# Layer norm gate moved between a selective scan and its product on VectorE

## Chip, cores and metric

The kernel runs on one core of a Trainium2 chip. The metric is the device time of one execution in microseconds. Times of the kernel before are given as the median of three runs; one more execution was profiled.

## Reference

The input is x of shape (2, 256, 256, 128) in float32. Two layers follow, each on the group-normalised x and each added to it. The first is a row attention; the change does not touch it. The second is a selective scan model with 256 inner channels, 16 states and 65,536 tokens per image:

```python
xz = x @ in_proj_w.T
xi, z = jnp.split(xz, 2, axis=-1)
xi = jax.nn.silu(conv3x3_depthwise(xi) + conv_b)
...
# selective_scan, for each channel d and state n along the tokens:
h = dA_t * h + dBx_t
y_t = sum over n of h * c_t
...
y = (y - mu) * jax.lax.rsqrt(var + 1e-05) * ln_g + ln_b     # over the 256 channels
y = y * jax.nn.silu(z)
return y @ out_proj_w.T
```

## The kernel before

The attention comes first (lines 269 to 575) and leaves its sum in DRAM. The second layer is the scan stage. It goes through 128 **steps** (64 per image); a step covers R = 4 rows of 256 tokens, that is T = 1024 tokens.

A step has NU = 32 **units**. The 128 partitions of a unit hold 32 channels times 4 states. The 32 units are 8 groups of channels times 4 groups of states. For unit t the engines do this, each with one instruction:

- `decay(t)` (line 958, ScalarE): da = exp(delta * a), into PSUM. There are two buffers, da0 and da1.
- `drive(t)` (line 968, GpSimd): hb = du * bb, for two units at once.
- `scan(t)` (line 980, VectorE): h = da * h + hb along the tokens. For most units it writes h over da in PSUM; for pooled units it writes h over hb in SBUF.
- `product(t)` (line 995, VectorE): yc = h * cc. In the five pooled pairs, which start at units 6, 14, 22, 26 and 30, the product is done on GpSimd for the pair (line 1004); unit 11 has its product on GpSimd alone.
- `add_up(t)` (line 1027, TensorE): for every four units, 32-column matmuls that add the states of yc into y in PSUM. It frees the yc buffers; the pool has four pairs.
- `remember(t)` (line 985, ScalarE): copies the last column of h to the state kept for the next step.

So VectorE runs scan, product, scan, product, with two scans and no product at a pooled pair.

Between the units run pieces of two other jobs. `project(k)` prepares a later step: transposes, the convolution as nine matmuls (line 678), the gate z (line 704), silu of both, and softplus. ScalarE does each silu or softplus as one pass of 2048 elements with a table load on both sides; they stand at units 12 (softplus, line 765), 20 (silu of z, line 720) and 28 (silu of xs, line 697). `finish_row` finishes one row of the step before, four rows per step, eight units apart. Its pieces, counted from the row's first unit a, a multiple of 8, are:

- a: `fetch` loads xres and szr (the silu of z) from DRAM, issued by SP.
- a: `turn` (line 830, TensorE) transposes and centres y into yt.
- a + 1 to a + 3: `stats`, `scales` and `norm` on ScalarE (lines 842 to 854) make the normalised row yn.
- a + 4: `back` (line 865, TensorE) transposes yn into yd in PSUM.
- a + 5: `gated` (line 873, VectorE): yg = yd * szr, 128 x 512.
- a + 7: `mix` (lines 877 and 881, TensorE) multiplies with the output projection and adds the residual.
- a + 8: `leave` (line 891, ScalarE) copies the row out, and SP stores it.

The gates of the four rows thus fall at units 5, 13, 21 and 29 of a step, none of them pooled, and each followed by a pooled pair at units 6, 14, 22 and 30. There are 512 gates.

The order on each engine is the order in which the loop at the end issues the pieces; no scheduler changes it within an engine. In a turn of that loop the scan and the product of unit t come first, then the pieces put at t with `at`, those for TensorE last. So the gate stood behind the product of its unit.

## Time and profile before

| what | value |
|---|---|
| median of three runs | 15883.89 us |
| lowest and highest run | 15882.23 and 15885.26 us |
| profiled execution, its own time | 15886.66 us |
| profiled execution, its span | 15884.8 us |
| scan stage in the profiled execution | from about 2680 us to the end |

The profile gives for each engine the time in which it was busy and, for each instruction, its start, its duration and what ended the idle time before it. In a timeline row the first number is the start in microseconds from the start of the span and the second the duration; brackets hold idle time ahead of the instruction and its releaser. In a row of stretches the busy times of the five engines (PE, PEld, DVE, ACT, POOL) are followed by the granted TensorE clock as a share of full speed, the DMA share and GB/s. DVE is VectorE, ACT ScalarE, POOL GpSimd, PE TensorE and PEld its weight load. A row of waits names who waited for whom, the microseconds in total, the number of times and the longest.

### The profile page before, as it was taken

What the parts mean: (1) busy time and instruction counts of PE and PEld (TensorE: products, weight loads), DVE (VectorE), ACT (ScalarE), POOL (GpSimd) and SP (SyncE); (2) the same over time, 40 slices, a digit from 0 to 9 for tenths busy, and PEclk for the clock granted to TensorE, in tenths of its full rate; (3) what the DMA queues carried; (4) which work ended last, traced back from release to release, by engine and by line L of the source; (5) the groups of instructions that cost most, each with busy time, mean ns of one, the idle gap of its engine ahead of it and who ended that gap; (6) DMA issues with size and microseconds to landing.
All of it is one profiled execution on the core that took longest, in us unless ns stands there. A gap on an engine that the chain in (4) does not pass through costs nothing. (4 is left out here: it accounts for less than half of the span.)

```text
span 15884.8 us, 178043 instructions
## 1 busy us (share of the span) xinstructions
PE 13780.9 (87%) x59451; PEld 7002.8 (44%) x59451; DVE 14454.8 (91%) x12356; ACT 10796.7 (68%) x20003; POOL 13328.8 (84%) x3344
## 2 busy tenths in 40 slices
PE   6999998888888888888888888888888888888886
PEld 4877884333333333333333333333333333333333
DVE  7665555999999999999999999999999999999998
ACT  3555554777777777777777677777777777777775
POOL 1111113999999999999999999999999999999998
PEclk8999998999999999999999999999999999999998
DMA  4322222767677767677777667777677767776675
GB/s 188 123 101 86 80 96 105 239 238 245 240 241 242 246 240 240 240 245 241 243 242 244 230 241 242 242 244 244 240 241 241 245 241 243 242 244 240 240 243 185
DMA packets 1428908, 3452.13 MB, mean 217 GB/s; under 512 B 119785, under 2 KB 711185, under 8 KB 1407505
## 3 DMA queue, kind: packets, MB, share of 16 engines
q1 hardware_dynamic: 1427984, 3440.73, 62.6%
q8 instruction: 468, 7.67, 0.2%
q14 instruction: 456, 3.73, 0.1%
HBM read 2752.41 MB, written 687.88 MB: 217 GB/s over the span
## 5 line engine op out<-in xcount | busy, mean ns | idle before, releaser
L968 POOL TENSOR_TENSOR hb<-du_r,bb 128x2048 f32<-128x2048 f32 x2048 | 9243.5, 4545 | 82.3 <-DMA du_r<-du_d 15.7
L980 DVE TENSOR_TENSOR_SCAN da<-da,state,hb 128x1024 f32<-128x1024 f32 x2688 | 6300.4, 2344 | 137.9 <-ACT da L958 134.3
L958 ACT ACTIVATE da<-delta_r,a_neg 128x1024 f32<-128x1024 f32 x4096 | 4580.7, 1118 | 88.9 <-DMA delta_r<-delta_d 10.1
L678 PE MATMUL u_ps<-xn,w_tap 128*128 128x512 f32 x9216 | 4335.3, 612 | 91.3 <-ACT sz L715 73.2
L995 DVE TENSOR_TENSOR yc<-da,cc 128x1024 f32<-128x1024 f32 x2688 | 3291.8, 1225 | 235.9 <-PE y L1027 69.1
L980 DVE TENSOR_TENSOR_SCAN hb<-da,state,hb 128x1024 f32<-128x1024 f32 x1408 | 3233.4, 2334 | 61.5 <-ACT state L985 47.7
L1004 POOL TENSOR_TENSOR yc<-hb,cc 128x2048 f32<-128x2048 f32 x640 | 2909.0, 4545 | 101.0 <-ACT state L985 81.1
L678 PEld LDWEIGHTS u_ps<-xn,w_tap 128*128 128x128 f32 x9216 | 1713.7, 195 | 2453.6 <-issue 1837.9
L1027 PE MATMUL y<-yc,sel 128*32 128x512 f32 x16384 | 2323.6, 689 | 18.5 <-POOL yc L1004 18.1
L435 POOL TENSOR_TENSOR x1g<-xc,bo_all 128x512 f32<-128x512 f32 x256 | 316.0, 1276 | 1840.5 <-DVE stats L484 1839.6
L985 ACT COPY state<-da 128x1 f32<-128x1 f32 x2688 | 425.9, 158 | 1637.5 <-DVE yc L995 1630.1
L830 PE MATMUL yt<-centre,ys 128*128 128x256 f32 x4096 | 1030.9, 395 | 284.7 <-ACT ob L891 284.7
L1027 PEld LDWEIGHTS y<-yc,sel 128*32 128x32 f32 x16384 | 470.2, 121 | 1790.0 <-issue 1646.5
L704 PE MATMUL z_ps<-xn,w_z 128*128 128x512 f32 x1024 | 696.3, 768 | 547.0 <-ACT xn L665 307.3
L746 PE MATMUL dt_ps<-xd,w_dt 8*128 8x512 f32 x1024 | 740.6, 811 | 482.0 <-ACT delta L757 385.6
L385 ACT ACTIVATE e<-s_ps,nmx 128x256 f32<-128x256 f32 x1024 | 477.6, 476 | 967.7 <-DVE nmx L376 960.0
L985 ACT COPY state<-hb 128x1 f32<-128x1 f32 x1408 | 268.5, 191 | 1242.7 <-DVE hb L980 1242.6
L830 PEld LDWEIGHTS yt<-centre,ys 128*128 128x128 f32 x4096 | 742.0, 191 | 464.4 <-ACT ob L891 381.9
L881 PE MATMUL o_ps<-w_out,szr 128*128 128x128 f32 x4096 | 793.9, 276 | 0.0
L881 PE MATMUL o_ps<-w_out,yg 128*128 128x128 f32 x4096 | 792.8, 275 | 0.0
L352 DVE TENSOR_TENSOR v<-v_ps,bv_all 128x512 f32<-128x512 f32 x256 | 177.1, 692 | 592.1 <-PE v_ps L345 592.1
L775 POOL TENSOR_TENSOR xs<-delta,xs 128x1024 f32<-128x1024 f32 x256 | 606.7, 2370 | 99.1 <-ACT delta L765 99.1
(134 smaller groups left out, 17280.7 us busy)
## 6 DMA issues: line engine op xcount, KB each, us to landing
bb<-bc_d SPq DMA_DIRECT2D x1024, 512.0 KB, 4.0
cc<-bc_d SPq DMA_DIRECT2D x1024, 512.0 KB, 5.3
delta_r<-delta_d SPq DMA_DIRECT2D x1024, 512.0 KB, 6.3
du_r<-du_d SPq DMA_DIRECT2D x1024, 512.0 KB, 5.2
sz_d<-sz SPq DMA_DIRECT2D x128, 1024.0 KB, 6.5
szr<-sz_d SPq DMA_DIRECT2D x512, 256.0 KB, 4.1
xs_d<-xs SPq DMA_DIRECT2D x128, 1024.0 KB, 9.5
xr<-xs_d SPq DMA_DIRECT2D x256, 512.0 KB, 5.9
```

The costliest lines, as they stand in the source:

```text
L678: nc.tensor.matmul(o["u"], w_tap[:, h, tap, :], xn[:, i * RB + dy : i * RB + dy + RB, dx : dx + W], start=(tap == 0), stop=(tap == 8),)
L704: nc.tensor.matmul(o["z"], w_z[:, h, :], xn[:, 1 + i * RB : 1 + (i + 1) * RB, 1 : W + 1], start=True, stop=True,)
L746: nc.tensor.matmul(o["dt"], w_dt[:, h, :], o["xd"][0:DR, i * TB : (i + 1) * TB], start=True, stop=True,)
L830: nc.tensor.matmul(o["yt"][:, j, :], ys[k, h][:, t0 + j * P : t0 + (j + 1) * P], centre[:, (1 - h) * P : (1 - h) * P + DI], start=(h == 0) ...
L881: nc.tensor.matmul(o["o"][:, j, :], o[by][:, h, j * P : (j + 1) * P], w_out[:, i, h, :], start=False, stop=(j == WT - 1 and h == NH - 1 an ...
L958: nc.scalar.activation(da, spreads["delta", k, h, q], AF.Exp, scale=a_neg[:, g, m : m + 1])
L968: nc.gpsimd.tensor_tensor(hb, spreads["pair", k, h, q], repeats["bb", k, h, m].unsqueeze(1).to_broadcast([P, 2, T]), ALU.mult,)
L980: nc.vector.tensor_tensor_scan(u["h"], u["da"], u["hb"], st, ALU.mult, ALU.add)
L985: nc.scalar.copy(st, units[t]["h"][:, T - 1 : T])
L995: eng.tensor_tensor(u["yc"], u["h"], repeats["cc", k, h, m], ALU.mult)
L1004: nc.gpsimd.tensor_tensor(yc, hb, repeats["cc", k, h, m].unsqueeze(1).to_broadcast([P, 2, T]), ALU.mult)
L1027: nc.tensor.matmul(y[q * CQ : (q + 1) * CQ, cols], sel, units[t + q]["yc"][:, cols], start=False, stop=(m == NSG - 1),)
```

## The change

The gate is no longer put into the list of pieces at its unit. It is kept in a dictionary `between`, and the loop calls it after the scan of that unit and ahead of its product. On VectorE the order scan, product, gate becomes scan, gate, product at the 507 gates that have a scan in their unit. For the last five rows there are no more scans, and their gates run alone, as before.

```diff
@@ -605,6 +605,7 @@
     slots = {}
+    between = {}
 
     def at(t, piece, *args, pe=False):
...
@@ -901,11 +902,11 @@
             (2, scales),
             (3, norm),
             (4, back),
-            (5, gated),
             (7, mix),
             (8, leave),
         ):
             at(a + i, piece, pe=piece in (turn, back, mix))
+        between[a + 5] = gated
 
@@ -1068,6 +1069,9 @@
                 decay(t + 1)
             if 0 <= t < end:
                 scan(t)
+            if t in between:
+                between[t]()
+            if 0 <= t < end:
                 if not pooled(t):
                     product(t)
             others, on_pe = slots.pop(t, ((), ()))
```

## Prediction

> **What bounds the kernel now.** I read the page's busy table first, then the waits of VectorE, then its timeline through one step of 32 units, and last the granted TensorE clock in short stretches. Below, "unit n" is the unit with t % 32 = n. A step has four gate products, at units 5, 13, 21 and 29, and there are 128 steps (127 of them with gates among scans).

> ```profile
> PE 13780.9 (87%) x59451; PEld 7002.8 (44%) x59451; DVE 14454.8 (91%) x12356; ACT 10796.7 (68%) x20003; POOL 13328.8 (84%) x3344
> ...
> DVE   7665555999999999999999999999999999999998
> ```

> VectorE is the fullest engine and is full from slice 8 on: that is the scan stage, where the change lies. GpSimd is nearly as full there, but VectorE waits for it hardly at all. The waits of VectorE, of which the scan stage shows these:

> ```profile
> DVE yc L995 <- PE y L1027: 69.1, 129, 2.2
> DVE hb L980 <- ACT state L985: 47.7, 126, 1.0
> DVE yg L873 <- PE yd L865: 43.8, 5, 10.7
> ```

> Two waits come once in every step (129 and 126 times). The gate's own wait for TensorE comes 5 times, all but nothing of it among the scans. The timeline of VectorE and TensorE around a gate at unit 13:

> ```profile
> 8055.84 2.35 DVE L980 TENSOR_TENSOR_SCAN da<-da,state,hb 128x1024 f32<-128x1024 f32 x1
> ...
> 8058.13 0.60 PE L865 MATMUL yd<-ident,yn 128*128 128x128 f32 x4
> 8058.22 1.23 DVE L995 TENSOR_TENSOR yc<-da,cc 128x1024 f32<-128x1024 f32 x1
> ...
> 8059.36 0.68 DVE L873 TENSOR_TENSOR yg<-yd,szr 128x512 f32<-128x512 f32 x1
> ...
> 8059.96 2.34 DVE L980 TENSOR_TENSOR_SCAN hb<-da,state,hb 128x1024 f32<-128x1024 f32 x1
> ```

> Scan to product is 2.38 us, product to gate 1.14, gate to the next scan 0.60: 4.12 in all. The product needs the scan's output and starts after its end. Where the next instruction is independent it starts ahead of the end: the scans of a pooled pair follow each other after 2.26 us (8059.96 to 8062.22). So the dependence costs 2.38 - 2.26 = 0.12 us. TensorE ends yd at 8058.73, 2.89 us after the scan's start and 0.63 us ahead of the gate.

> The wait for y, at unit 28, in three steps (VectorE's timeline):

> ```profile
> 8003.16 1.23 DVE L995 TENSOR_TENSOR yc<-da,cc 128x1024 f32<-128x1024 f32 x1 [0.31 <-PE y L1027]
> ...
> 8105.56 1.22 DVE L995 TENSOR_TENSOR yc<-da,cc 128x1024 f32<-128x1024 f32 x1 [0.31 <-PE y L1027]
> ...
> 8209.45 1.23 DVE L995 TENSOR_TENSOR yc<-da,cc 128x1024 f32<-128x1024 f32 x1 [1.45 <-PE y L1027]
> ```

> The first two are 102.40 us apart. So are most steps to within 0.01 us, which no sum of engine times would give. TensorE's clock says why; the stretches before, in and after its two slow patches of a step:

> ```profile
> 7998.41:8001.83 3.42, 3.21 (x10) 0.90 (x14) 3.42 (x2) 3.11 (x8) 3.42 (x2) 0.50 1.00 338
> 8001.83:8005.24 3.41, 3.41 (x17) 1.17 (x10) 3.10 (x3) 3.38 (x3) 3.41 (x2) 1.00 0.58 180
> 8042.79:8046.20 3.41, 2.04 (x6) 0.69 (x5) 3.38 (x3) 2.61 (x7) 3.33 (x2) 1.00 0.41 121
> 8046.21:8056.44 10.23, 8.64 (x23) 2.00 (x22) 10.04 (x7) 8.52 (x14) 10.15 (x4) 0.50 0.73 249
> 8056.45:8059.86 3.41, 3.41 (x13) 1.68 (x12) 3.38 (x3) 3.32 (x6) 3.41 (x1) 1.00 0.95 303
> ```

> The third column from the right is the granted clock: half speed for 3.4 us ahead of unit 28's y and for 10.2 us ahead of unit 13's yd, full speed around them.

> [...] half-clock stretches of 3.42 and 10.23 us are one and three windows, and 102.40 us is exactly 30 windows. So the step is locked to the clock's windows. [...]

> How the lock works, from the scan starts of all steps. If a step begins later against the windows, TensorE does more of unit 28's y at full clock, and VectorE's wait for it shrinks by half of the shift; if earlier, it grows by half. After a disturbance of 0.35 us (about every 16 steps) the wait jumps to 1.45 us, and the steps take 103.89, 103.35, 102.88, 102.64, 102.52, 102.46, 102.43, 102.41 us: the excess over 102.40 halves each time and sums to 3.4 us, one window. There are 7 or 8 such slips. The wait adds to VectorE's work whatever is missing from 30 windows. yd of unit 13 moves likewise: in those steps it ended 1.48 to 3.13 us after the scan's start.

> **The change, part by part.** Nothing is added or removed: on VectorE 507 of the 512 gates swap places with the product before them; the orders of TensorE, ScalarE, GpSimd and SP stay. SP's szr load loses a wait for VectorE that had long been met: nothing. TensorE's y takes an extra wait for that product, which ended several units earlier: nothing, since that work covers it. SP's szr load (4.1 us to land, issued five units or some 17 us ahead) is there before an earlier gate; if it were not, the gate would hold VectorE for the rest. The product ends 0.60 - 0.12 = 0.48 us later after its scan; behind it wait ScalarE's state copy and decay t+2 (1.12 us), due 2.26 us after the next scan starts: covered, with some 0.9 us left.

> A scan into PSUM followed by an independent instruction does not occur in this trace. Bounds for its pitch: 2.26 us (pooled pair, gain 0.12) and 2.38 (gain 0). No reason excludes a small loss, but the gate has no tie to the scan; I take 2.26.

> - Unit 5: yd is over 3 us early. 2.26 + 0.60 + 1.14 = 4.00 for 4.12: -0.12 us a step.
> - Unit 21: the next scan is held by ScalarE (the 47.7 us): the decay of unit 22 runs from 8085.61 to 8086.73 at the end of a ScalarE chain that began at product 19 (silu and two table loads lie in it), and the scan starts at 8086.83. Saved time becomes wait: 0.
> - Unit 29: yd ends at 8006.32, 0.2 us ahead of 8004.30 + 2.26, where the gate would start: no wait. The next scan's decay ends at 8008.27, and scans start 0.10 us after at the earliest, against 8008.42 now: -0.05; -0.12 once unit 28's wait is longer.
> - Unit 13: yd comes at 2.89, the gate at 2.93 (0.05 from TensorE's end to VectorE's start at unit 28), the product at 3.53, the next scan at 4.67: +0.55 us if the windows stay where they are.

> Sum at today's phase: 0.55 - 0.12 - 0.05 = +0.38 us a step. But then a step is longer than 30 windows and drifts against them. Carrying the halving rules for yd and y from step to step, the drift ends where unit 13's yd is early enough (its scan start plus 1.5 us; the gate is free from 2.2 on) and unit 28's wait has grown. There units 5, 13 and 29 each save 0.12, and the wait at unit 28 grows from 0.24 above its shortest form to 0.24 + 0.36 = 0.60, which lies within the 0.1 to 1.35 seen. The step is again **102.40 us**. The rules give 8 full slips: about +3 us in all.

> Sum against the profiled execution's 15886.66 us (span 15884.8 and 1.9 around it): 15889.6. It lies 2.8 above the median of 15883.89, so I give **15886** for the runs.

> **Rivals.**
> - The late yd stays (slower). Place: gate at unit 13; price +0.38 us x 127 = +48: 15932. It decides if yd ends later than 2.22 us after its scan's start in most steps, or if steps slip a window every 8 instead of 16 (8 more slips x 3.4 = +27: 15911). For it: at today's phase yd is 0.64 late. Against: yd moves with the windows. 13%.
> - The lock breaks (faster): 0.36 x 127 = -46, 15838. It needs y to come earlier with the gates. Against: y hangs on the clock, and the wait took every value from 0.1 to 1.35 while the rest of the step stayed the same. 7%.
> - The swap saves nothing, since the gate too starts 2.38 after the scan: then unit 28's wait stays near 0.24 and the step is again 102.40: 15886. Same number, another mechanism; 15% within the 80%.

> **Numbers.** A measurement tells 0.2%, 32 us, from no change. Within: 80%, slower 13%, faster 7%. The range takes slips lost (7 x 3.4 = 24 below) and ten added (34 above): 15856 to 15920; it leaves out most of the two outer rivals.

> **What would show it.** Right: steps of 102.40 us; a scan at units 5 and 13 followed by the gate after 2.26 us; VectorE's wait for y near 0.7 us at unit 28, some 110 us in total; no regular wait of yg for yd; the wait for ScalarE at unit 22 up by 0.12 a step. The slow patch ahead of unit 13 begins some 0.6 us later after unit 8's scan. Wrong: yg waiting for yd in most steps, steps off 102.40, or slips much more or less often than every 16 steps.

## Result, and the profile after

The changed kernel takes **15856.1 us** (median of 20 runs, 15852.0 to 15861.7) against 15883.7 for the kernel before (20 runs, 15878.4 to 15890.0): a ratio of **0.9982, 95% interval 0.9977 to 0.9988**, 27.6 us or 0.17% faster. The profiled execution took 15853.44 us, its span is 15851.4 against 15884.8.

The busy line of the page and the waits of VectorE that answer to those shown of before:

```profile
PE 13783.1 (87%) x59451; PEld 6983.3 (44%) x59451; DVE 14400.7 (91%) x12356; ACT 10834.7 (68%) x20003; POOL 13333.6 (84%) x3344
```

```profile
DVE yc L996 <- PE y L1028: 90.0, 125, 1.4
DVE hb L981 <- ACT state L986: 65.2, 126, 1.0
DVE yg L874 <- PE yd L866: 45.4, 6, 10.7
```

VectorE is busy 54 us less and waits 38 us more: 21 us more for TensorE's y (69.1 before) and 17 more for ScalarE (47.7 before). The pauses too short to be listed as waits take 17 us less, which with the two others makes the 33 us of span. Among the scans the gate waits for yd once, 0.47 us in step 87 (the first step is step 0). The timeline of VectorE and TensorE around unit 13:

```profile
8039.68 2.35 DVE L981 TENSOR_TENSOR_SCAN da<-da,state,hb 128x1024 f32<-128x1024 f32 x1
8040.66 0.60 PE L866 MATMUL yd<-ident,yn 128*128 128x128 f32 x4
...
8041.93 0.67 DVE L874 TENSOR_TENSOR yg<-yd,szr 128x512 f32<-128x512 f32 x1
...
8042.52 1.21 DVE L996 TENSOR_TENSOR yc<-da,cc 128x1024 f32<-128x1024 f32 x1
8043.66 2.35 DVE L981 TENSOR_TENSOR_SCAN hb<-da,state,hb 128x1024 f32<-128x1024 f32 x1
```

The gate starts 2.25 us after the scan, the product 0.59 later, the next scan 1.14 later: 3.98 us where it was 4.12. And yd now ends 1.58 us after the scan's start (8041.26), where it ended 2.89 after. The product of unit 28 in three steps:

```profile
7987.29 1.23 DVE L996 TENSOR_TENSOR yc<-da,cc 128x1024 f32<-128x1024 f32 x1 [0.72 <-PE y L1028]
...
8089.69 1.23 DVE L996 TENSOR_TENSOR yc<-da,cc 128x1024 f32<-128x1024 f32 x1 [0.72 <-PE y L1028]
...
8192.26 1.23 DVE L996 TENSOR_TENSOR yc<-da,cc 128x1024 f32<-128x1024 f32 x1 [0.56 <-PE y L1028]
```

The first two are again 102.40 us apart, and the wait is 0.72 where it was 0.31: every step takes back what its gates saved. The third is a step with the disturbance of 0.35 us. Before, its wait jumped from 0.31 to 1.45 and a **slip** followed, a step and its successors that together take one clock window more. (A **window** is a measured pitch: in the profile of before the granted clock is 1.00 or 0.50, and all 300 whole stretches at 0.50 begin on one grid of 3.4133 us, to within 1 ns, and last one or several such pitches; 30 of them are 102.40 us.) Now the wait takes up half of the disturbance (0.72 to 0.56), the step is 102.57 us, and the next steps of 102.33, 102.35 and 102.38 us give the rest back.

So where did the 33.4 us of span go? I summed, from the starts of the unit 0 scans, what each step is above 102.40 us:

| steps | before | after |
|---|---|---|
| 1 to 60 | +17.5 us | -0.4 us |
| 61 to 63 (change of image) | +20.1 us | +17.3 us |
| 64 to 126 | +11.1 us | +1.6 us |
| steps over 102.95 us | 20 | 3 |

The first and the third row lose 27.4 us, and most of that are **slips that no longer happen**: eight before (steps 5, 14, 21, 37, 53, 79, 95 and 111), one after (step 87), so seven windows or 23.9 us. The last three steps give 2.0 of the 27.4. A further 2.8 lie at the change of image, the rest of the 33.4 at the two ends. The quiet steps did not become shorter by anything. The granted clock even fell, from a mean of 0.929 to 0.925 over the span.

The regular disturbance is the same in both kernels: VectorE pauses for 0.44 to 0.47 us between a scan and its product, at unit 12 in steps 5, 21, 37 and 53, at unit 18 in steps 79, 95 and 111. All seven brought a slip before, none does after. In step 53 of the changed kernel it reads:

```profile
8141.29 1.23 DVE L996 TENSOR_TENSOR yc<-da,cc 128x1024 f32<-128x1024 f32 x1 [0.44 <-issue]
```

The slip at step 87 began otherwise: the product of unit 12 waited 1.08 us for y, and the gate of unit 13 then waited for yd.

The stretches at half clock (granted clock 0.50) in one step of the changed kernel:

```profile
8030.75:8037.57 6.82, 4.80 (x18) 1.09 (x18) 6.72 (x4) 5.50 (x11) 6.82 (x3) 0.50 0.67 219
8058.06:8061.47 3.41, 3.41 (x14) 0.60 (x16) 3.38 (x3) 2.46 (x5) 3.41 (x1) 0.50 1.00 357
8081.95:8088.77 6.82, 4.35 (x17) 1.10 (x18) 6.82 (x4) 6.12 (x13) 6.82 (x2) 0.50 1.02 360
```

Two, one and two windows, where this step had three and one before: a new one at unit 18, and two windows for one ahead of unit 28. The stretch ahead of unit 13 now ends at 8037.57, 2.11 us ahead of the scan's start, where it ended 0.60 us behind it (8056.44 and 8055.84), and yd is early.

### The profile page after: what moved, and what is told of

Read it like the earlier page. It is cut to its first block, busy times and chain, and to the rows that moved or that the text cites. A ratio compares the mean times of both kernels' runs of the same rounds, so it can differ in the third digit from the quotient of the medians.

```text
span 15851.4 us, 178043 instructions
## 1 busy us (share of the span) xinstructions
PE 13783.1 (87%) x59451; PEld 6983.3 (44%) x59451; DVE 14400.7 (91%) x12356; ACT 10834.7 (68%) x20003; POOL 13333.6 (84%) x3344
## 5 line engine op out<-in xcount | busy, mean ns | idle before, releaser
L679 PE MATMUL u_ps<-xn,w_tap 128*128 128x512 f32 x9216 | 4233.1, 600 | 13.6 <-ACT sz L716 8.9
L679 PEld LDWEIGHTS u_ps<-xn,w_tap 128*128 128x128 f32 x9216 | 1670.3, 190 | 2277.4 <-issue 1852.5
L1028 PE MATMUL y<-yc,sel 128*32 128x512 f32 x16384 | 2414.0, 714 | 17.8 <-POOL yc L1005 17.0
L705 PE MATMUL z_ps<-xn,w_z 128*128 128x512 f32 x1024 | 761.3, 835 | 633.9 <-ACT sz L716 324.8
L747 PE MATMUL dt_ps<-xd,w_dt 8*128 8x512 f32 x1024 | 695.1, 764 | 511.2 <-ACT delta L758 419.4
```

The lines of the kernel that those rows point to most:

```text
L679: nc.tensor.matmul(o["u"], w_tap[:, h, tap, :], xn[:, i * RB + dy : i * RB + dy + RB, dx : dx + W], start=(tap == 0), stop=(tap == 8),)
L705: nc.tensor.matmul(o["z"], w_z[:, h, :], xn[:, 1 + i * RB : 1 + (i + 1) * RB, 1 : W + 1], start=True, stop=True,)
L747: nc.tensor.matmul(o["dt"], w_dt[:, h, :], o["xd"][0:DR, i * TB : (i + 1) * TB], start=True, stop=True,)
L1028: nc.tensor.matmul(y[q * CQ : (q + 1) * CQ, cols], sel, units[t + q]["yc"][:, cols], start=False, stop=(m == NSG - 1),)
```

## Experiments

**Theory 1**: the step is held at 30 windows of TensorE's clock, and the gain is the slips avoided, because the step rests at another point against the windows. **Theory 2**: VectorE's work sets the time, and each of the 507 swaps gives its own share, 27.6 / 507 = 0.054 us. They part as soon as the gates are swapped at one unit only, since theory 2 then gives a quarter each time.

The kernel before was run again beside each group of experiments and took 15883.7 to 15887.9 us there. The ratios are to those runs; between kernels of different groups, a few microseconds say nothing.

### Gates swapped at one unit only

For U = 5, 13, 21 and 29:

```diff
-        between[a + 5] = gated
+        if (a + 5) % NU == U:
+            between[a + 5] = gated
+        else:
+            at(a + 5, gated)
```

> Only the gates of unit 5 stand between scan and product; those of units 13, 21 and 29 stay behind the product. Theory 1 (the step is held at 30 windows of TensorE's clock, 102.40 us, and the whole gain of the change is the window slips that no longer happen): 0.15 us saved a step moves the step 0.3 us away from the point where a disturbance of 0.35 us makes it slip, so almost no slips are left and the whole gain is there: 22 to 28 us below the kernel before, steps still 102.40. Theory 2 (each swap saves its own share, 27.6 us / 507 gates = 0.054 us): 127 x 0.054 = 7 us below.

> Only the gates of unit 13 stand between scan and product. Theory 1: the step has no resting point, because where VectorE's work and the wait at unit 28 would make 102.40 us, yd comes 0.6 us too late for the gate; steps slip a window every two to four steps and the time is 50 to 90 us above the kernel before (slower by 0.3 to 0.6%), with yg waiting for yd in most steps. Theory 2: 7 us below the kernel before.

> Only the gates of unit 21 stand between scan and product. Theory 1: the next scan is held by ScalarE, so the step, its phase and its slips stay as they were: within 3 us of the kernel before. Theory 2: 7 us below.

> Only the gates of unit 29 stand between scan and product. Theory 1: as for unit 5, 20 to 28 us below the kernel before with almost no slips, steps 102.40. Theory 2: 7 us below.

| swapped at | time us | ratio to before (95%) | steps over 102.95 us |
|---|---|---|---|
| unit 5 | 15858.4 | 0.9983 (0.9976 to 0.9989) | 5 |
| unit 13 | 15957.9 | 1.0046 (1.0033 to 1.0058) | 61 |
| unit 21 | 15884.3 | 0.9999 (0.9991 to 1.0007) | 20 |
| unit 29 | 15861.9 | 0.9986 (0.9979 to 0.9992) | 8 |
| all | 15856.1 | 0.9982 (0.9977 to 0.9988) | 3 |

Theory 2 falls. Unit 5 alone gives 26.9 us, the whole gain; unit 29 alone 23.3; unit 21 nothing, and VectorE's wait for ScalarE is 65.7 us there for 47.7; and the same saving at unit 13 costs 72.7 us. The sign depends on the place. With unit 5 alone the wait of unit 28 rests at 0.45 us, and the disturbance takes it to 0.27 without a slip; from 0.31, in the kernel before, the same disturbance brings the slip. With unit 13 alone, the gate waits for yd 38 times in all, 33 of them among the scans, where the kernel before has none and the changed one a single one. The waits of VectorE and the timeline of one such step:

```profile
DVE yc L999 <- PE y L1031: 133.0, 128, 2.2
...
DVE yg L874 <- PE yd L866: 68.6, 38, 9.8
```

```profile
6843.22 2.35 DVE L984 TENSOR_TENSOR_SCAN da<-da,state,hb 128x1024 f32<-128x1024 f32 x1
...
6845.67 0.60 PE L866 MATMUL yd<-ident,yn 128*128 128x128 f32 x4
...
6846.31 0.69 DVE L874 TENSOR_TENSOR yg<-yd,szr 128x512 f32<-128x512 f32 x1 [0.74 <-PE yd L866]
...
6848.04 2.34 DVE L984 TENSOR_TENSOR_SCAN hb<-da,state,hb 128x1024 f32<-128x1024 f32 x1
```

yd ends 3.05 us after the scan's start, so the gate starts 3.09 us after its scan instead of 2.25 (0.74 us of it idle), and the next scan 4.82 us after it instead of 4.12. The steps run 104.25, 103.29, 102.85, 102.63 us and again from the start. The four sum to 413.02 us, which is 121 windows where 120 would be four quiet steps: one slip every four steps. In three of the four the gate does not wait at all; a step of 102.40 us has no place to rest, because where the wait at unit 28 would make it (some 0.45 us), yd ends 3.0 us after the scan, in the kernel before and with unit 5 alone as well. That explains why 33 waits of 0.7 us, 24 us in all, can cost 73: most of it comes as the wait for y, 133.0 us for 69.1, in the same step (1.45 us) and in the next three.

### All but unit 13

```diff
-        between[a + 5] = gated
+        if (a + 5) % NU == 13:
+            at(a + 5, gated)
+        else:
+            between[a + 5] = gated
```

> The gates of units 5, 21 and 29 stand between scan and product, those of unit 13 behind the product. Theory 1: VectorE's work is 0.14 us a step longer than in the changed kernel, and the wait at unit 28 is that much shorter; steps 102.40 us, few slips, 15856 within 6 us. Theory 2: three quarters of the gain, 15863.

Measured: 15854.1 us, ratio 0.9979 (0.9971 to 0.9987), quiet steps of 102.40. The swap at unit 13, harmful alone, gives and takes nothing beside the others that these runs can tell: without it the wait at unit 28 rests at 0.59 us, with it at 0.72.

### Less VectorE work: half a gate

The gate of unit 5 leaves out half of its columns; for these the output projection takes szr in place of yg, so that the other engines keep their work. Once in the changed kernel, once in the kernel before with all gates behind their products:

```diff
-            nc.vector.tensor_tensor(o["yg"], o["yd"], o["szr"], ALU.mult)
+            if (a + 5) % NU == 5:
+                nc.vector.tensor_tensor(
+                    o["yg"][:, 0, :], o["yd"][:, 0, :], o["szr"][:, 0, :], ALU.mult
+                )
+            else:
+                nc.vector.tensor_tensor(o["yg"], o["yd"], o["szr"], ALU.mult)
...
-                    for i, by in enumerate(("yg", "szr")):
+                    first = "szr" if h and (a + 5) % NU == 5 else "yg"
+                    for i, by in enumerate((first, "szr")):
```

> The changed kernel, whose gate at unit 5 computes only its first 256 of 512 columns (in those rows the output projection takes szr in place of yg for the other half): some 0.3 us less work on VectorE in every step. Theory 1 (step held at 30 windows): the wait for y at unit 28 grows by those 0.3 us, steps stay 102.40 us, and the time is that of the changed kernel, 15856 within 5 us. Theory 2 (VectorE's work sets the time): 127 x 0.3 = 38 us less than the changed kernel, 15818.

> The kernel before, all gates behind their products, whose gate at unit 5 computes only its first 256 of 512 columns (the output projection takes szr for the other half in those rows): some 0.27 us less VectorE work a step. Theory 1: the order of gate and product is not what counts; any tenth of a microsecond saved moves the step away from its slip point: 15850 to 15860, 24 to 34 us below the kernel before, steps 102.40. Theory 2: 127 x 0.27 = 34 us below, 15850, with steps of 102.13.

The changed kernel with half a gate: 15849.9 us (ratio 0.9978, 0.9970 to 0.9987), 6 us below the changed kernel where the work saved is 127 x 0.27 = 34 us; it is also 1 us below the range that theory 1 gave. Two successive quiet steps of it on VectorE's timeline:

```profile
6963.18 1.23 DVE L1002 TENSOR_TENSOR yc<-da,cc 128x1024 f32<-128x1024 f32 x1 [0.98 <-PE y L1034]
...
7065.57 1.23 DVE L1002 TENSOR_TENSOR yc<-da,cc 128x1024 f32<-128x1024 f32 x1 [0.98 <-PE y L1034]
```

Again 102.39 apart, and the wait is up from 0.72 to 0.98: the 0.26 us saved lie in it. Summed as above, its steps are 3.9 us shorter in all, in and after the disturbed ones.

The kernel before with half a gate: 15855.1 us (0.9980, 0.9972 to 0.9988), median step 102.398, four steps over 102.95 instead of 20. The time alone fits both theories; the steps decide, since theory 2 wants 102.13. So the order of gate and product is not what counts. Savings of 0.15 to 0.7 us a step that reach the product of unit 28 and meet no late yd brought 23 to 34 us, with little regard to their size.

### More VectorE work: one reduction

```diff
                     product(t)
+                if t % NU == 2:
+                    nc.vector.tensor_reduce(spin, centre[:, 0:P], AX.X, ALU.add)
```

> The changed kernel with one more VectorE instruction a step: a reduction of 128 constant columns behind the product of unit 2, some 0.15 to 0.2 us. Theory 1: the step's resting point moves 0.3 to 0.4 us, past the point where yd of unit 13 comes a window's share later; the gate then waits, and the step slips every four or five steps: 40 to 70 us above the kernel before, that is 70 to 95 us above the changed kernel for 20 to 25 us of work. Theory 2: 20 to 25 us above the changed kernel, about 15879.

Measured: 15945.4 us, ratio to before 1.0038 (1.0026 to 1.0051): 89 us above the changed kernel. The reduction makes unit 2 longer by 0.19 us (3.79 for 3.60), 24 us in all. Where no disturbance comes between, its steps run 104.36, 103.17, 102.79, 102.59, 102.50 and again; the five sum to 515.41 us, 151 windows for 150: a slip every five steps. The gate waits for yd 29 times at unit 13. The waits of VectorE:

```profile
DVE yc L997 <- PE y L1029: 130.0, 127, 1.5
...
DVE yg L875 <- PE yd L867: 65.5, 33, 9.8
```

### TensorE's idle gaps filled

In the kernel before the clock fell at TensorE's idle gaps of units 9 and 10 and of units 25 and 26. That the gaps make it fall was my estimate from these places. If so, and if the clock is the cause of the lock, filling the gaps must break it. Matmuls of zero weights (`nought` is a tile of zeros) add 0 to the open sum y:

```diff
+        def busy(t, n, cols):
+            if 0 <= t < len(steps) * NU:
+                for _ in range(n):
+                    nc.tensor.matmul(
+                        outs["y"][0:CQ, 0:cols], nought,
+                        w_tap[:, 0, 0 : cols // P, :], start=False, stop=False,
+                    )
+        for t, times_, cols in (
+            (2, 2, 512), (25, 1, 256), (26, 1, 512), (49, 1, 512), (50, 1, 512)
+        ):
+            at(base + t, busy, base + t, times_, cols, pe=True)
...
         for r in range(0, n, RB):
             t = base + r // RB
+            if r:
+                at(t, busy, t, 2, 512, pe=True)
             at(t, turn, "raw", r, min(RB, n - r), pe=True)
```

The second version has `(41, 1, 256)` and `(42, 2, 512)` in the list as well, and leaves the matmuls out up to unit 5 of the first step.

> The changed kernel with added matmuls of zero weights into y (they add 0 to it) in TensorE's idle gaps at units 9, 10, 17, 18, 25 and 26, some 6.5 us a step, so that its clock is not halved. Theory 1: no lock is left; VectorE's wait for y at unit 28 all but goes, steps are about 102.07 us (the next scan at unit 30 is then held by ScalarE), and the time is 15820 (15810 to 15835), faster than both kernels. Theory 2: TensorE is off the path; 15856, or slower by the added TensorE work.

> The kernel before with the same added matmuls. Theory 1: no slips, steps about 102.35 us: 15857 (15850 to 15865), some 35 us above the changed kernel with the same matmuls, which is what the moved gates are worth when nothing else holds the step. Theory 2: 15884, 27 us above the changed kernel with the same matmuls.

> The changed kernel with the added matmuls of after_warm and two more sets in TensorE's idle gaps at units 1 and 2, where its clock was still halved for one window a step. Theory 1: the last half-clock stretches go; VectorE's own sum, about 101.8 us, and GpSimd's 101.7 us of work are left: steps of 101.8 to 101.95, 15800 to 15815. If GpSimd alone already holds after_warm, nothing more is gained: 15820.

| kernel | time us | ratio to before (95%) | median step |
|---|---|---|---|
| before, matmuls added | 15836.2 | 0.9970 (0.9958 to 0.9981) | 102.19 |
| changed, matmuls added | 15820.3 | 0.9960 (0.9947 to 0.9974) | 102.05 |
| changed, more matmuls added | **15809.7** | **0.9952 (0.9939 to 0.9964)** | 102.05 |

TensorE does more, the granted clock over the profiled execution rises (0.963 for 0.929 in the kernel before, 0.966 and 0.970 for 0.925 in the changed one), both kernels get faster, and the steps no longer rest at 102.40 us: the lock is the clock. In the kernel before, the product of unit 28 started 2.64 us after its scan in a quiet step; with the matmuls it starts after 2.43. That is 0.21 us less, and the step is 102.19.

The gaps at which the clock fell are short: in the kernel before no gap of a quiet step was over 2.6 us (1.4 and 1.6 at units 9 and 10, 2.4 and 2.6 at units 25 and 26), and the clock fell at both pairs. In the window of 3.41 us ahead of each fall TensorE was busy for 2.04 us (8042.79 to 8046.20) and 0.66 us (7994.99 to 7998.40), so it was at work ahead of both. How much idle time it takes to make the clock fall, these runs do not show. One stretch of the scan stage, 4000 to 15000 us, in the kernel before, and then in the changed kernel with more matmuls:

```profile
4000.00:15000.00 11000.00, 9512.78 (x38519) 4267.12 (x38517) 10745.60 (x6099) 7854.90 (x13696) 10873.28 (x2571) 0.93 0.70 242
```

```profile
4000.00:15000.00 11000.00, 10188.09 (x41098) 4396.17 (x41096) 10778.34 (x6135) 7903.89 (x13774) 10938.55 (x2588) 0.98 0.71 243
```

The clock is 0.98 for 0.93, and the fifth busy time, GpSimd's, is 99.4% of the stretch (98.8% before). VectorE's waits in that kernel, over the span, and then GpSimd's in the stretch:

```profile
DVE yg L894 <- PE yd L886: 52.5, 36, 10.7
DVE hb L1001 <- ACT state L1006: 47.0, 123, 1.0
...
DVE da L1001 <- POOL hb L989: 10.4, 58, 0.4
...
DVE yc L1016 <- PE y L1048: 2.0, 5, 0.6
```

```profile
POOL yc L1025 <- PE y L785: 11.3, 1, 11.3
POOL yc L1025 <- ACT state L1006: 3.7, 3, 1.8
POOL hb L989 <- DVE da L1001: 3.7, 2, 2.3
POOL yc L1025 <- PE y L1048: 0.8, 1, 0.8
```

The wait for y is gone (2.0 for 90.0). Without it a step of the changed kernel would be 102.40 - (3.05 - 2.43) = 101.78 us; the shortest steps are that, but the median is 102.05. VectorE now waits for GpSimd's hb, 58 times, and GpSimd itself waits for others only 19.5 us in the 11000, 11.3 of them at once (73.5 in the kernel before). It runs at its own pace: GpSimd is what comes next. The gate, too, waits for yd 26 times in this stretch, 6.9 us in all. The second set left the median step where it was; its 11 us lie in the long steps. With the change of image left out, the first version has 28 steps over 102.2 us, 13.0 us above it in all, the second 4 and 2.0 us.

Some expectations were missed here. For the kernel before I expected steps of 102.35 and 15857 us, from a ScalarE chain that would hold unit 30; the steps are 102.19 and the time 15836, so that chain does not hold them. The swap is therefore worth 16 us between the two kernels with the first set, not 35: in the changed one GpSimd, which waits for others 23.2 us in the stretch, holds it back. And the second set was to bring steps of 101.8 to 101.95.

## Why the prediction failed

The lock, the resting step and the wait at unit 28 came as predicted; the number of slips did not. The step at fault is one sentence: **"The rules give 8 full slips: about +3 us in all."** There was one (at step 87), against eight before, and the time fell by 27.6 us. Point by point:

- Saved per gate: 0.12 us taken, from the pitch of a pooled pair. Measured 0.147 at units 5 and 29, 0.135 at 13. The gate itself takes 0.67 for 0.68 us, and the product, which no longer follows its scan, 1.21 for 1.23.
- Unit 21: 0 predicted; only21 gives 0. The wait for ScalarE rose by 17 us in all; 127 x 0.12 = 15 was predicted.
- Unit 13: the +0.55 us "if the windows stay where they are" is what a kernel without the other swaps shows: +0.70, where yd ends 3.05 us after the scan and not 2.89, and the waiting gate holds the product and the scan behind it. In the changed kernel yd moved out of the way, as predicted: 1.59 measured at rest, 1.5 predicted.
- Unit 28: 0.60 above the wait's shortest form predicted; from scan to product it is 3.06 us for 2.43, so 0.63 measured, and the quiet step is 102.40 us as predicted. The total was to be 110 us and is 90.0, about 125 times 0.72 us, with next to no slips in it.
- The slow stretch ahead of unit 13: 0.6 us later after unit 8's scan predicted, 0.7 measured (7.58 for 6.87). That it lasts two windows instead of three, that a new one stands at unit 18, and that the one ahead of unit 28 lasts two, was not foreseen.
- **Slips**: the mis-sized term is the distance from the resting point to the point of slipping, the place where yd of unit 13 jumps to a late end. The prediction prints only what came of it. I had yd at 1.50 us at rest and the jump at 1.42: the 3.13 us seen behind the jump, less half a window (1.71), by a slope of exactly one half. But the steps quoted in the prediction end at 1.48. As half of each shift is passed on (after a slip the excess of three steps in a row was 0.48, 0.24 and 0.12 us), my figures are 2 x (1.50 - 1.42) = 0.16 us of phase. Measured at rest is 1.587, and in the trace of before the last yd ahead of the jump ends at 1.484, so the distance is 2 x (1.587 - 1.484) = 0.21 us. A disturbance of 0.35 us arrives at the next step as 0.17 to 0.21, since unit 28's wait takes the rest: over the edge by my number, just inside it by the measured one. An error of 0.05 us in a phase decided over 25 us of time. That all seven stayed inside is a matter of hundredths: the largest left yd at 1.49. Step 87, where another delay made yd late, shows that a late yd does bring a slip.
- The range: its lower end does not follow from its own terms, as 15886 - 24 is 15862 and not 15856. The measured 15856.1 lies at that end only by this error.

Of the rivals, "the swap saves nothing" is refuted by the 2.25 us pitch. "The late yd stays" is real, but is the fate of unit 13 alone. "The lock breaks" did not happen, and happens when TensorE's gaps are filled.

Still open is what makes VectorE pause about every 16 steps. For the same pause the profile names no releaser ("issue") in some steps, and in others TensorE's y or the scan itself; no run was made on it. The margin of 0.21 us is read from the traces; no run shifted it alone.

## What to carry to other kernels

Here steps had the same length to a hundredth of a microsecond, and that length, 102.40 us, was 30 clock windows. A saving on the busiest engine became a wait (0.26 us less at unit 5 took the wait at unit 28 from 0.72 to 0.98), and what could be won was how often the step slips (23 to 34 us) and what holds the lock (another 36 to 46 us in the changed kernel). To tell whether another kernel is held in this way, look for a wait that comes once in every step and grows by just what was saved, and for steps whose excess sums to one pitch of the clock's changes. Then test by shortening or lengthening one instruction by a known amount: if the time does not follow the work, in size or in sign, try filling the gaps of the engine whose clock falls before moving anything else.
